# Local attention with whitening on one Trainium2 core: part of the last moments moved among the output tiles, outputs written over consumed inputs, larger stores

## The chip, the cores and the metric

The kernel runs on one core of a Trainium2 chip. The metric is device time in microseconds (us) of one execution; the kernel before has a median of 672.0 us in three runs. Profiles come from the hardware profiler, one execution each.

## What is computed

Layer 0 turns x (4 images, 256 channels, 64 x 64 pixels, float32) into 49 attention weights for each pixel and sums 49 shifted copies of x with them. Layer 1 whitens the result in groups of 64 channels.

```python
k = conv(x, w1, dilation=2, padding=6) + b1          # 256 -> 128 channels, 7x7
k = conv(k, w2) + b2                                 # 128 -> 49, 1x1
attn = softmax(k, axis=1)
y = einsum('bkchw,bkhw->bchw', 49 shifted copies of x, attn)
# layer 1: 4 groups of 64 channels, m = all pixels of all images
mean = y.mean(-1); xc = y - mean
Sigma = EPS * I + xc @ xc.T / m
rTr = 1 / trace(Sigma);  P = I
for _ in range(5):
    P = 1.5 * P - 0.5 * (P @ P @ P) @ (Sigma * rTr)
out = (P * sqrt(rTr)) @ xc * weight + bias
```

No output can be written before the moments (the sums of y and of y times y transposed) of all pixels of a channel group are known. Everything after that point is the end stage of the kernel, and the change lies around it.

## The kernel before, in words

**Layout.** Channels lie on the 128 partitions, in two channel halves, cc = 0 and cc = 1, of two groups of 64 each. An image b lies in two buffers (`slots[2*b + pr]`), one for each parity pr of the row; a buffer is `[128, cc, 32, 64]` float32, so one channel half of it is 8 KB on each partition. y is written over x in these buffers.

**Work before the end.** For most of the run TensorE computes the convolution (line 604). Attention goes by 16 steps n = (image, row parity, column parity). Each step brings a band of weights from memory (lines 1208 and 1220), turns x on TensorE (`make_blocks`, line 1264, evicted to `xb` or `xbs` and, for the edges, `xbz`, lines 1286 and 1295), sums with matmuls (`weighted_sum`, line 1328), and evicts y into the buffer (`store_y`, line 1350; for the last step `store_part`, lines 1363 and 1364). y is then turned (`turn_y`, line 1400, copied to `yt` at line 1410; for parts of the last step `turn_part`, lines 1372 and 1380) and multiplied into the moments (`moment`, line 1419, tile `sig`), 8 turned pieces of each channel half for each half of a step. LAST is step 15, `prev` step 14. The second half of `prev` is turned and summed while LAST's first half is computed: two calls of `turn_y`, four transposes each, and one call of `moments`, for both channel halves at once.

**Whitening.** `whiten(cc)` is a generator, one for each channel half. A `next` on it issues one step: mean and trace (lines 1743 to 1753), the two matmuls with `blk` and the scaled covariance (1758 to 1772), then four iterations of two steps (a product of P with P and S, copied by ScalarE to `sq` at line 1780; a product of the two halves of `sq`, taken into P by VectorE at lines 1785 and 1786), then `wmx` and the scale, then the offset: twelve `next` calls in all. The generator of cc = 0 runs first, without stop. Between its steps, `fill` takes eleven entries from `units`, a list of TensorE work on the second channel half of LAST: sums, evictions, turns, moments.

**Output tiles.** `idx` counts 33 tiles: cc = 0, then cc = 1; in each the images 3, 2, 1, 0; in each four tiles of 8 rows of each parity (the very first is split in two). A tile takes eight matmul instructions of `parts_mm` (line 1730), four for each parity, into a pair of PSUM banks. Three pairs rotate, named `apply`, `cv` and `tp` in the profile; `tp` is shared with turns and whitening steps. ScalarE evicts one parity (line 1859), VectorE the other (line 1865), with scale and offset, into a staging tile `out` (six of them rotate), and SyncE issues a store of 512 KB (line 1871), 4 KB for each partition. The two entries of `units` that are left after the first whitening, moments of LAST, come behind the matmuls of tiles 1 and 2. The second whitening starts behind tile 4 (`LEAD`) and takes one step behind the matmuls of each tile from tile 6 on.

**What sets the order.** Every TensorE instruction around the change goes through `pe(...)`, which keeps program order on TensorE. VectorE and ScalarE are ordered by the compiler's scheduler within their dependences; `tc.high_priority()` and `tc.issue_after(x)` bend this (the first step of the second whitening is held behind the two evictions of tile LEAD). Stores go in program order on SyncE.

Of the kernel before, what the change touches and what calls it, by code (L numbers as in the profile page):

```python
# [9 lines left out]
F32 = mybir.dt.float32  # L10
# [22 lines left out]
def kernel(  # L33
# [29 lines left out]
    nc = tc.nc  # L63
    B, C, H, W = x.shape
    P = 128
# [32 lines left out]
    def pe(ins):  # L98
        return tc.keep_in_program_order(ins)
# [9 lines left out]
    def tp():  # L109
        return ps_tp.tile([P, 512], F32, tag="tp", name="tp")  # L110
# [20 lines left out]
    slots = {}  # L131
    store = []

    def halves(t):

        return t.rearrange("p c r w -> p c (r w)").rearrange(
            "p c (h r w) -> p c h r w", h=2, r=SH
        )
# [3 lines left out]
    def read_x(o, k, queue):  # L142
        b, pr = divmod(k, 2)
        for cc in range(NCC):
            src = x[b, cc * P : (cc + 1) * P].rearrange("c (r two) w -> c r two w", two=2)
            for h in range(2):
                yield queue.dma_start(o[:, cc, h], src[:, :, pr, h * SW : (h + 1) * SW])  # L147
# [33 lines left out]
    t = tp()  # L181
# [3 lines left out]
    t = tp()  # L185
# [5 lines left out]
    for k in range(2):  # L191
        t = ps_cv.tile([P, 512], F32, name=f"cv{k}")
# [53 lines left out]
    for k, c0 in enumerate(range(0, P, CB)):  # L246
        n = min(CB, P - c0)
        t = cv_buf[k % 2]
# [15 lines left out]
    for k0 in range(0, KT, TB):  # L264
        n = min(TB, KT - k0)
        t = tp()
# [835 lines left out]
    def place(n):  # L1102

        b, k = divmod(n, 4)
        return (b, k % 2, k // 2) if b == B - 1 else (b, k // 2, k % 2)
# [135 lines left out]
    def tile_of(t, cc, t8, h, pc):  # L1241

        return halves(t)[:, cc, h, TR8 * t8 : TR8 * (t8 + 1), bass.ds(pc, TC, 2)]

    def turned_by(n):

        return swap if place(n)[1] else ident

    def where(n):

        b, h, pc = place(n)
        return slots[2 * b + h], pc

    upper_edge = []
    LAST = 4 * B - 1
# [107 lines left out]
                return nc.vector.tensor_scalar(o, i, shift, None, ALU.add)  # L1363
            return nc.scalar.activation(o, i, AF.Identity, bias=shift)

    def turn_part(half, cc, k, to=None, on=nc.scalar.copy):

        yt, pc = where(LAST)
        t = tp()
        for h in range(2):  # L1370
            pe(
                nc.tensor.transpose(
                    t[:, h * P : (h + 1) * P],
                    tile_of(yt, cc, 2 * half + k, h, pc),
                    turned_by(LAST),
                )
            )
        yb = yt_buf[k][:, :, cc if to is None else to]
        with tc.high_priority():
            on(yb[:, :, :, :GW], t[:, :C].rearrange("p (h g c) -> p h g c", h=2, c=GW))  # L1380
        for h in range(2):
            turned_part[half, cc, 2 * k + h] = yb[:, h]

    turned_part = {}

    def moments_part(half, cc, pieces=range(4), end=False):

        for k in pieces:
            moment(turned_part[half, cc, k], cc, end and k == 3)

    count = [0]
    ybs = {}
# [1 line left out]
    def turn_y(n, t8):  # L1394
        yt, pc = where(n)
        t = tp()
        for h in range(2):
            for cc in range(NCC):
                pe(
                    nc.tensor.transpose(  # L1400
                        t[:, h * C + cc * P : h * C + (cc + 1) * P],
                        tile_of(yt, cc, t8, h, pc),
                        turned_by(n),
                    )
                )
        yb = yt_buf[t8 % NY]
        for h in range(2):
            ybs[n, 2 * t8 + h] = yb[:, h]
        with tc.high_priority():
            return nc.scalar.copy(  # L1410
                yb.rearrange("p h a g c -> p (h a g) c")[:, :, :GW],
                t[:, : 2 * C].rearrange("p (e c) -> p e c", c=GW),
            )

    def moment(yb, cc, end=False):

        for g in range(P // GW):
            pe(
                nc.tensor.matmul(  # L1419
                    sig[g * GW : (g + 1) * GW, cc],  # L1420
                    yb[:, g, :GW],
                    yb[:, g],
                    start=(count[0] == 0),
                    stop=end,
                    skip_group_check=True,
                )
            )
        count[0] += 1

    def moments(n, half):  # L1430

        for i in range(4 * half, 4 * half + 4):
            for cc in range(NCC):
                moment(ybs[n, i][:, cc], cc)
# [149 lines left out]
    pieces = read_x(halves(store[4]), 4, nc.sync)  # L1584
# [34 lines left out]
    rpool = ctx.enter_context(tc.tile_pool(name="rp", bufs=1, reuse_waits="tile"))  # L1619
# [24 lines left out]
    n = 4 * last_b  # L1644
# [21 lines left out]
    def sums(half, cc, *ks):  # L1666
        for k in ks:
            weighted_sum(LAST, half, k, (cc,))

    prev = open_n.pop()  # L1670
    turn_y(prev, 2)
    sums(0, 0, 0)
    make_blocks(LAST, 1)
    sums(0, 0, 1)
    make_blocks(LAST, 2)
    sums(0, 0, 2)
    turn_y(prev, 3)
    sums(0, 0, 3, 4)
    stored = store_part(0, 0)
    make_blocks(LAST, 3)  # L1680
    moments(prev, 1)
    root = work.tile([P, 1], F32, tag="root", name="root")
    with tc.issue_after(stored.ins):
        nc.scalar.activation(root, cmask[:, :1], AF.Sqrt)
# [10 lines left out]
    units = [  # L1695
        lambda: sums(0, 1, 2, 3),
        lambda: (sums(0, 1, 4), store_part(0, 1)),
        lambda: sums(1, 1, 0, 1, 2),
        lambda: sums(1, 1, 3),
        lambda: (sums(1, 1, 4), store_part(1, 1, True)),  # L1700
        lambda: turn_part(0, 1, 0),
        lambda: turn_part(0, 1, 1),
        lambda: turn_part(1, 1, 0, 0),
        lambda: turn_part(1, 1, 1, 0),
        lambda: moments_part(0, 1, (0, 1)),
        lambda: moments_part(0, 1, (2, 3)),
        lambda: moments_part(1, 1, (0, 1)),
        lambda: moments_part(1, 1, (2, 3), True),
    ]


# [15 lines left out]
    def parts_mm(t, lhs, rhs, crossed=False):  # L1727
        for i, o in ((G0, G1 if crossed else G0), (G1, G0 if crossed else G1)):
            pe(
                nc.tensor.matmul(  # L1730
                    t[o], lhs[i], rhs[i], start=True, stop=True, skip_group_check=True
                )
            )
# [81 lines left out]
    chains = [whiten(cc) for cc in range(NCC)]  # L1815
# [3 lines left out]
    NT = 512  # L1819
    TR = NT // W  # L1820

    LEAD = 4
    evicted = {}

    def bank_pairs():
        while True:
            yield [ps_y.tile([P, NT], F32, tag="y", name="apply") for _ in range(2)]
            yield cv_buf
            yield [tp(), tp()]

    pair = bank_pairs()
    idx = -1
    for cc in range(NCC):
        for b in (3, 2, 1, 0):
            rows = [(q, TR) for q in range(0, SH, TR)]
            if (cc, b) == (0, B - 1):
                rows[:1] = [(0, TR // 2), (TR // 2, TR // 2)]
            for k, (r0, nr) in enumerate(rows):
                idx += 1
                st = rpool.tile([P, TR, 2, W], F32, tag="out", name=f"out_{b}_{cc}_{r0}", bufs=6)  # L1840
                st = st[:, :nr]
                ts = next(pair)
                for pr in range(2):
                    y = halves(slots[2 * b + pr])[:, cc, :, r0 : r0 + nr, :]
                    parts_mm(
                        ts[pr][:, : nr * W],
                        (wmx if pr else wm)[cc],
                        y.rearrange("p h r w -> p h (r w)"),
                        crossed=pr == 1,
                    )  # L1850
                if idx in (1, 2):
                    units.pop(0)()
                if idx > LEAD + 1:
                    next(chains[1], None)
                for pr in range(2):
                    o = st[:, :, pr, :].rearrange("p r (h w) -> p h r w", h=2)
                    i = ts[pr][:, : nr * W].rearrange("p (h r w) -> p h r w", h=2, w=SW)
                    if pr == k % 2:
                        on_act = nc.scalar.activation(
                            o, i, AF.Identity, bias=beta[cc], scale=sc[cc]  # L1860
                        )
                    else:
                        behind = evicted.get(idx - 1) if idx <= LEAD else None
                        with tc.issue_after(behind.ins) if behind else nullcontext():
                            evicted[idx] = nc.vector.tensor_scalar(
                                o, i, sc[cc], beta[cc], ALU.mult, ALU.add
                            )
                if idx == LEAD:
                    with tc.issue_after(evicted[idx].ins), tc.issue_after(on_act.ins):
                        next(chains[1])  # L1870
                nc.sync.dma_start(
                    out[b, cc * P : (cc + 1) * P, 2 * r0 : 2 * (r0 + nr), :],
                    st.rearrange("p r two w -> p (r two) w"),
                )
# [31 lines left out]
```

## Time and profile before

| what | value |
|---|---|
| median of three runs (lowest, highest) | 672.0 us (671.94, 672.1) |
| the profiled execution's own time | 671.98 us |
| its span | 670.2 us |
| granted TensorE clock, mean | 0.995 |
| PE busy in the span | 647.1 us, 97% |
| DVE, ACT busy | 566.5 us, 332.6 us |
| stores issued at line 1871 | 31 of 512 KB, 2 of 256 KB; first issued at 624.0 us, last at 663.0 us |
| packets in the window 622 to 671 on the queue of the stores | 4752, 16.78 MB |

PE is TensorE's matmuls, PEld its weight loads, DVE is VectorE, ACT is ScalarE, SPq is SyncE's queue. The span runs from the first to the last recorded event. The DMA share of a stretch is the mean busy share of the core's 16 DMA engines; it can come out slightly above 1. A view by windows gives busy time by engine in each stretch, then the granted TensorE clock, the DMA share and GB/s. The chain of waits follows the work that ended last back through what released it; with a window it is listed in order of time as start, length, what. The timeline lists instructions in order of time with, in brackets, the idle time before and what ended it. In the trace a float32 matmul shows as two instructions and a transpose as one.

### The profile page before, as it was taken

The numbers are of one execution on the slowest core, as the hardware profiler recorded it, in microseconds if no ns is written. First come the engines' busy times: TensorE is split into PE (matmuls) and PEld (weight loads), VectorE is DVE, ScalarE is ACT, GpSimd is POOL, SyncE is SP. The second block draws the span as 40 slices with busy tenths as digits, with TensorE's granted clock in tenths as the row PEclk, the third lists the DMA queues.
The fourth block names the chain that finished last, engine by engine and source line by source line (L and its number), as shares of the span: only waits on it lengthen the run. The fifth ranks groups of instructions, "written<-read, shape, count | busy, mean of one in ns | idle before, by whom it ended". The sixth has DMA issues, their size and how long they took to land.

```text
span 670.2 us, 19064 instructions
## 1 busy us (share of the span) xinstructions
PE 647.1 (97%) x7800; PEld 527.4 (79%) x7800; DVE 566.5 (85%) x1240; ACT 332.6 (50%) x862; POOL 115.0 (17%) x173
## 2 busy tenths in 40 slices
PE   6999999999999999999999999999999999999993
PEld 1439673357899998889999998999999999997430
DVE  3699999899399889999999789989999988634773
ACT  1424331023465556467755563464855566635663
POOL 0000551662203002001022020002130203500000
PEclk9999999999999999999999999999999999999998
DMA  8961899994499989313587773027374325749698
GB/s 314 251 172 66 133 242 376 218 195 68 113 195 231 209 270 314 112 53 94 167 275 246 233 276 106 2 68 193 97 189 123 71 64 117 192 103 371 255 404 347
DMA packets 110991, 126.09 MB, mean 188 GB/s; under 512 B 69255, under 2 KB 92344, under 8 KB 109752
## 3 DMA queue, kind: packets, MB, share of 16 engines
q1 hardware_dynamic: 94104, 69.35, 35.9%
q0 software_dynamic: 10752, 37.26, 21.6%
q10 hardware_dynamic: 6048, 18.27, 8.9%
q8 instruction: 61, 1.00, 0.6%
q14 instruction: 26, 0.21, 0.1%
HBM read 78.78 MB, written 52.36 MB: 196 GB/s over the span
## 4 chain that ended last, share of the span: by engine, by line
PE 83%; DVE 10%; DMA 2%; ACT 2%; issue 1%; SPq 0%; POOL 0%; DVEq 0%; ACTq 0%; POOLq 0%
PE cv L604 30%; PE y L1328 13%; PE cv L779 10%; PE acc L779 9%; PE sig L1419 5%; PE tp L1400 4%; PE tp L1264 4%; PE cv L251 2%; DMA out_dram<-out 2%; PE tp L1730 2%; DVE zz L352 1%; DVE pv L352 1%; PE tp L1021 1%; DVE zz L348 1%; DVE ct L352 1%
## 5 line engine op out<-in xcount | busy, mean ns | idle before, releaser
L604 PE MATMUL cv<-xh,wr 128*49 128x128 f32 x4160 | 232.3, 273 | 0.1
L604 PEld LDWEIGHTS cv<-xh,wr 128*49 128x49 f32 x4160 | 226.1, 124 | 2.9 <-issue 1.0
L1158 POOL DMA_DIRECT2D sd<-zt x120 | 63.0, 532 | 295.0 <-ACT zt L1139 232.0
L1328 PE MATMUL y<-band,xb 128*128 128x209 f32 x448 | 93.7, 341 | 0.6 <-ACT xb L1295 0.6
L1328 PEld LDWEIGHTS y<-band,xb 128*128 128x128 f32 x448 | 75.8, 191 | 1.4 <-ACT xb L1295 0.8
L615 ACT COPY pv<-cv 113x486 f32<-113x486 f32 (+2 forms) x60 | 26.0, 433 | 84.6 <-PE cv L604 84.2
L352 DVE SCALAR_TENSOR_TENSOR pv<-pv 113x162 f32<-113x162 f32 x176 | 53.4, 326 | 1.5 <-ACT pv L615 0.9
L1410 ACT COPY yt<-tp 128x512 f32<-128x512 f32 x60 | 35.0, 592 | 24.3 <-PE tp L1400 23.5
L1139 ACT COPY zt<-d 32x112 f32<-32x112 f32 (+2 forms) x132 | 38.6, 292 | 11.7 <-DVE d L1009 5.8
L1400 PE MATMUL tp<-ident,slot 128*128 128x128 f32 x240 | 41.3, 296 | 0.2 <-ACT slot L1350 0.2
L1061 ACT ACTIVATE d<-tp,mx 128x49 f32<-128x49 f32 x96 | 27.5, 323 | 27.4 <-DVE mx L1058 20.7
L1264 PE MATMUL tp<-ident,slot 128*128 128x128 f32 x256 | 40.5, 282 | 0.0
L1419 PE MATMUL sig<-yt 128*64 128x65 f32 x1024 | 38.0, 225 | 0.9 <-ACT yt L1410 0.9
L1400 PEld LDWEIGHTS tp<-ident,slot 128*128 128x128 f32 x240 | 34.9, 205 | 5.1 <-issue 3.8
L1264 PEld LDWEIGHTS tp<-ident,slot 128*128 128x128 f32 x256 | 38.2, 205 | 0.4 <-DMA sd<-zt 0.4
L1419 PEld LDWEIGHTS sig<-yt 128*64 128x64 f32 x1024 | 32.9, 137 | 6.8 <-issue 1.9
L1295 ACT COPY xb<-tp 128x512 f32<-128x512 f32 x52 | 30.6, 588 | 8.8 <-PE tp L1264 5.6
L779 PE MATMUL acc<-slot,tap 128*49 128x256 f32 (+7 forms) x224 | 34.7, 468 | 0.0
L352 DVE SCALAR_TENSOR_TENSOR xh<-ct 128x512 f32<-128x512 f32 x40 | 26.6, 694 | 5.7 <-PE cv L604 5.4
L779 PEld LDWEIGHTS acc<-slot,tap 128*49 128x49 f32 x224 | 16.1, 123 | 17.9 <-issue 15.5
L147 POOL DMA_DIRECT2D slot<-in_x_dram x12 | 20.4, 1699 | 53.3 <-DVE xh L352 38.2
L348 DVE TENSOR_TENSOR pv<-pv 113x162 f32<-113x162 f32 (+1 forms) x77 | 27.8, 369 | 0.3
(258 smaller groups left out, 1143.7 us busy)
## 6 DMA issues: line engine op xcount, KB each, us to landing
out_dram<-out SPq DMA_DIRECT2D x31, 512.0 KB, 5.8
band<-sd SPq DMA_DIRECT2D x64, 242.0 KB, 3.5
sd<-zt POOLq DMA_DIRECT2D x120, 77.0 KB, 3.9
wr<-gd ACTq DMA_DIRECT2D x14, 588.0 KB, 4.7
wr<-gd ACTq DMA_DIRECT2D x14, 490.0 KB, 4.4
slot<-in_x_dram POOLq DMA_DIRECT2D x12, 512.0 KB, 10.2
ahead<-in_x_dram POOLq DMA_DIRECT2D x12, 512.0 KB, 7.5
spill<-slot POOLq DMA_DIRECT2D x3, 2048.0 KB, 8.4
```

What stands on the lines that cost most here:

```text
L348: return in_turn(TT(o, a, b, ALU.subtract))
L352: return in_turn(STT(o, a, f, b, ALU.mult, ALU.add))
L604: nc.tensor.matmul(o, wv[:, sc, sr, cc], xv[bc][:, h * NCC + cc], start=(j == 0), stop=(j == len(terms) - 1), skip_group_check=True,)
L779: nc.tensor.matmul(ps[h * HB : h * HB + KT, :, o0:o1], w[v][:, cc], rhs, start=(j == 0 and k == 0), stop=(j == len(order) - 1), skip_group ...
L1139: ins = nc.scalar.copy(o, i)
L1158: dma = queue.dma_start(bass.AP(tensor=D.tensor, offset=D.offset + h * HS + g * RS, ap=[[LS, TC], [CR * RS, NCH], [1, KS * WS]],), zt[p0 : ...
L1264: nc.tensor.transpose(t[:, h * C + cc * P : h * C + (cc + 1) * P], tile_of(xt, cc, t8, h, pc), turned_by(n),)
L1295: (nc.vector.tensor_copy if n > 4 * B - 3 else nc.scalar.copy)(xb.rearrange("p a c -> p (a c)"), t[:, : 2 * C])
L1328: nc.tensor.matmul(y_ps[n, half, cc][:, q0 : q0 + nq, c0:c1], xb[:, cc * P : (cc + 1) * P], rhs, start=(k == 0), stop=(k == len(PIECES[hal ...
L1400: nc.tensor.transpose(t[:, h * C + cc * P : h * C + (cc + 1) * P], tile_of(yt, cc, t8, h, pc), turned_by(n),)
L1410: return nc.scalar.copy(yb.rearrange("p h a g c -> p (h a g) c")[:, :, :GW], t[:, : 2 * C].rearrange("p (e c) -> p e c", c=GW),)
L1419: nc.tensor.matmul(sig[g * GW : (g + 1) * GW, cc], yb[:, g, :GW], yb[:, g], start=(count[0] == 0), stop=end, skip_group_check=True,)
```

## The change

Five edits, all in the end stage:

1. Of the second half of `prev`, only the first channel half is turned and summed where it was; the second half's turns (`turn_part(1, 1, 0 and 1, n=prev)`) and moments become four more entries of `units`. The key of `turned_part` gets the step n.
2. `units` now has 17 entries. Eleven are taken in the first whitening as before; the other six are taken behind the matmuls of tiles 2 to 7: the turn by ScalarE, the turn by VectorE, two entries of LAST's moments, two of `prev`'s.
3. `LEAD` goes from 4 to 6. The second whitening starts behind tile 7 (LEAD + 1), and from tile 8 on there are two places for a step in each tile, one behind each parity's matmuls; two of every three places are used. What is left is run before cc = 1 begins.
4. Outputs of all but the first image of cc = 0 are evicted into the buffers of the image before (its channel half is consumed by then), not into the six rotating `out` tiles.
5. For cc = 1, two tiles make one store of 1 MB, 8 KB for each partition.

```diff
-    def turn_part(half, cc, k, to=None, on=nc.scalar.copy):
-        yt, pc = where(LAST)
+    def turn_part(half, cc, k, to=None, on=nc.scalar.copy, n=LAST):
+        yt, pc = where(n)
...
-            turned_part[half, cc, 2 * k + h] = yb[:, h]
+            turned_part[n, half, cc, 2 * k + h] = yb[:, h]
...
-    def moments_part(half, cc, pieces=range(4), end=False):
+    def moments_part(half, cc, pieces=range(4), end=False, n=LAST):
         for k in pieces:
-            moment(turned_part[half, cc, k], cc, end and k == 3)
+            moment(turned_part[n, half, cc, k], cc, end and k == 3)
...
     prev = open_n.pop()
-    turn_y(prev, 2)
+    turn_part(1, 0, 0, n=prev)
     sums(0, 0, 0)
...
-    turn_y(prev, 3)
+    turn_part(1, 0, 1, n=prev)
     sums(0, 0, 3, 4)
     stored = store_part(0, 0)
     make_blocks(LAST, 3)
-    moments(prev, 1)
+    moments_part(1, 0, n=prev)
...
         lambda: moments_part(0, 1, (2, 3)),
+        lambda: turn_part(1, 1, 0, n=prev),
+        lambda: turn_part(1, 1, 1, on=nc.vector.tensor_copy, n=prev),
         lambda: moments_part(1, 1, (0, 1)),
-        lambda: moments_part(1, 1, (2, 3), True),
+        lambda: moments_part(1, 1, (2, 3)),
+        lambda: moments_part(1, 1, (0, 1), n=prev),
+        lambda: moments_part(1, 1, (2, 3), True, n=prev),
     ]
...
-    LEAD = 4
+    LEAD = 6
...
-    idx = -1
+    idx, hops = -1, 0
+    free = []
     for cc in range(NCC):
+        if cc:
+            for _ in chains[1]:
+                pass
         for b in (3, 2, 1, 0):
+            outs = [
+                t.rearrange("p r w -> p (r w)").rearrange("p (r two w) -> p r two w", two=2, w=W)
+                for t in free[-2:]
+            ]
+            free += [slots[2 * b + pr][:, cc] for pr in range(2)]
...
-                st = rpool.tile([P, TR, 2, W], F32, tag="out", name=f"out_{b}_{cc}_{r0}", bufs=6)
-                st = st[:, :nr]
+                if outs:
+                    st = outs[k // 2][:, k % 2 * TR : k % 2 * TR + TR]
+                else:
+                    st = rpool.tile(
+                        [P, TR, 2, W], F32, tag="out", name=f"out_{b}_{cc}_{r0}", bufs=6
+                    )[:, :nr]
...
                         crossed=pr == 1,
                     )
-                if idx in (1, 2):
+                    if idx > LEAD + 1:
+                        if hops % 3 != 1:
+                            next(chains[1], None)
+                        hops += 1
+                if idx > 1 and units:
                     units.pop(0)()
-                if idx > LEAD + 1:
-                    next(chains[1], None)
...
-                if idx == LEAD:
+                if idx == LEAD + 1:
                     with tc.issue_after(evicted[idx].ins), tc.issue_after(on_act.ins):
                         next(chains[1])
+                if cc:
+                    if k % 2 == 0:
+                        continue
+                    st, r0, nr = outs[k // 2], r0 - TR, 2 * TR
                 nc.sync.dma_start(
```

More of the change, by code (lines that the diff above doesn't have):

```diff
@@ L1374, in turn_part @@
                     tile_of(yt, cc, 2 * half + k, h, pc),
-                    turned_by(LAST),
+                    turned_by(n),
                 )
```

## The prediction

> **What bounds the kernel now.** First the busy shares by slices: TensorE is at nine tenths nearly to the end, so up to the first store the run is TensorE's program, and after it the DMA share is high. So I read the end stage in windows of 1 us (columns: stretch, length, busy time of PE, PEld, DVE, ACT, POOL with counts, clock, DMA share, GB/s).
>
> ```profile
> 624.00:625.00 1.00, 1.00 (x16) 0.28 (x12) 0.44 (x1) 0.44 (x1) 0.00 (x0) 1.00 0.11 43
> 625.00:626.00 1.00, 1.00 (x16) 0.52 (x16) 0.67 (x1) 0.73 (x1) 0.00 (x0) 1.00 1.01 377
> 626.00:627.00 1.00, 1.00 (x16) 0.41 (x12) 0.47 (x2) 0.32 (x2) 0.00 (x0) 1.00 0.28 105
> 627.00:628.00 1.00, 1.00 (x16) 0.35 (x12) 0.82 (x2) 0.98 (x2) 0.00 (x0) 1.00 0.99 401
> ...
> 650.00:660.00 10.00, 8.98 (x60) 2.20 (x54) 6.43 (x8) 6.22 (x8) 0.00 (x0) 1.00 1.02 406
> ...
> 667.00:668.00 1.00, 0.00 (x0) 0.00 (x0) 0.00 (x0) 0.00 (x0) 0.00 (x0) 0.50 0.67 262
> ```
>
> The stores run at 406 GB/s, so 512 KB take 0.524288/0.406 = 1.291 us and all 16.78 MB 41.32 us. Bytes flow from about 624.87 (43 of 377 GB/s in the window before 625) to 667.65: 42.78 us. So the DMA engines lack work for only 1.46 us, most of it in the 626 window. The end is **first store, plus bytes over rate, plus gaps, plus 2.5 us of landing and closing**. What sets the first store is in the chain of waits:
>
> ```profile
> 602.35 0.68 PE tp L1400 x4
> ...
> 605.75 0.37 ACT xbz L1286
> 606.12 0.04 issue
> 606.17 0.46 PE y L1328 x2
> 606.63 0.49 PE tp L1264 x4
> 607.12 1.08 PE sig L1419 x32
> 608.20 0.68 PE tp L1372 x4
> ```
>
> TensorE's work, but for one wait on ScalarE's edge copies that ends at 606.17. The third view is the timeline of the output tiles:
>
> ```profile
> 623.77 0.45 PE L1419 MATMUL sig<-yt 128*64 128x65 f32 x8
> 624.15 0.65 PE L1730 MATMUL tp<-slot,PS 64*64 64x512 f32 x2
> ...
> 629.11 0.22 DVE L1753 SCALAR_TENSOR_TENSOR dg<-mu,nmu,dg 128x1 f32<-128x1 f32 x1
> 629.25 0.22 DVE L1764 SCALAR_TENSOR_TENSOR PS<-sig,eps 128x64 f32<-128x64 f32 x1
> 629.38 0.80 DVE L1865 TENSOR_SCALAR out<-tp,ab 128x512 f32<-128x512 f32 x1
> 630.10 0.80 DVE L1865 TENSOR_SCALAR out<-apply,ab 128x512 f32<-128x512 f32 x1
> 630.82 0.28 DVE L1765 SCALAR_TENSOR_TENSOR PS<-tp,mu,PS 128x64 f32<-128x64 f32 x1
> ```
>
> A store needs a tile each 1.291 us, and until about 642 tiles come each 1.2 to 1.4 us: the compute side has hardly a margin there, and whatever is put among these tiles can starve the stores. From 647 on evictions wait for stores (`out` free again); that backlog has no price.
>
> **What the Trainium skill says.** "DMA: Bandwidth & Descriptors", section "Where 436 GB/s comes from", gives 435.2 GB/s as the ceiling of the SBUF side. The trace agrees: 406 here with 4 KB rows in 512 KB, and 427.7 (mean of the windows 608 to 617) for the 2 MB loads `back<-spill` with 16 KB rows. Its section "Rules for kernel authors" asks for at least 1 MiB in a DMA; 406 at 512 KB says little is left to gain. Its section "Latency and other measured facts" has some 600 ns to the first byte; here tile 2's store issues at 626.21 and bytes come at 627.0, 0.8 us. "PSUM — Partial Sum Buffer", section "Engine vs sequencer instructions": ScalarE and VectorE are strict queues and matmuls run in program order. The trace shows it: the tile behind a whitening step waits with the step.
>
> **The change, part by part.** I work against the profiled execution: 671.98 us, span 670.2 (1.78 around it); the median is 672.0, the same within 0.1. Clock times of the new kernel are in the old clock; the shift of step 1 comes off at the end.
>
> *1. Half of `prev`'s turns and moments leave the path.* A `turn_y` is 0.47 us in the chain; the first, at 602.28, loses half: 0.235. The second stands in the wait for the edge copies and earns nothing; that wait itself starts from transposes behind the first turn, so it moves 0.235 too. The moments at 607.12 lose half of 1.08: 0.54. Sum **-0.775**, if nothing else is late: the turn at 608.20 would start at 607.43, and what it needs (ScalarE's y eviction, 606.67 to 607.40) ends at 607.17 when moved; the square-root table load and the `yt` copy behind it end near 608.95, the moments that need them come at 609.68. Both hold.
>
> *2. The units among the tiles.* No more unit behind tile 1, so tile 2 starts at once; behind tiles 2 to 7 stand two turns and four moments. Costs on TensorE: a moments unit 0.38 (623.84 to 624.22 in the chain), a tile next to other shapes 1.02, a plain tile 0.86. A turn of two transposes costs 0.235 alone and 0.44 with its change of shape in the first whitening; I take 0.44. Their copies (0.37 on ScalarE, 0.42 on VectorE) fit between evictions. Rule: an eviction ends 0.86 after its tile's matmuls (0.05 and 0.81), its store's bytes come 0.85 after that. Tile 1's matmuls end at 623.84. Tile 2: matmuls 624.86, bytes 626.57 (0.43 earlier than now). Then 0.44 + 1.02 twice and 0.38 + 1.02 three times: bytes of tiles 3 to 7 at 628.03, 629.49, 630.89, 632.29, 633.69. Each is 0.1 to 0.17 after the store before it is done: 1.40 us for a tile against 1.291. Tile 7's evictions end at 632.84, its store at 634.98.
>
> *3. The start of the second whitening.* It has one tile between its start and its first matmul now; then none. Behind tile 7's eviction VectorE needs 0.86 to line 1753 (628.47 to 629.33): 633.70. The matmul that waits for it stands between tile 8's two halves, so TensorE idles from 632.95, and the second half runs 634.05 to 634.50. Behind it are queued the rest of tile 8, all later tiles and the ScalarE eviction. Eviction to 635.36, bytes **636.21: 1.23 after the queue ran dry**. VectorE then does line 1764 (0.2), tile 8's eviction (0.8) and lines 1765 to 1772 (0.9, as 630.82 to 631.72): 635.6. The order is a guess from now, where an eviction goes ahead of 1765; the other order frees P 0.65 sooner and delays this eviction as much. So the first product in tile 9 starts at 635.75, tile 9 is evicted at 637.14, bytes **637.99, 0.49 after** the store before it.
>
> *4. The iterations.* Two of three half tiles carry a step. Per iteration: product, `sq` copy (0.27) behind whatever ScalarE evicts (0.78), product, VectorE's update (0.22) behind its eviction. Walking it through: first products at 635.75, 637.52, 639.6, 641.2, the last update at 643.05; TensorE waits once, about 0.55 in tile 11, whose bytes come at 640.83, **0.26 after** tile 10's. Then 1.2 us a tile keeps ahead of 1.291, so the six stores of tiles 11 to 16 end at 640.83 + 6 x 1.291 = 648.58. With the shift: **647.80**. Now: 667.65 - 20.66 (16 stores) = 646.99. The first half is 0.81 later although it starts 0.775 sooner.
>
> *5. Outputs over y, and the 1 MB stores.* No eviction waits for `out`, but the DMA engines were full then: nothing. Before the first 1 MB store two tiles must be out, 17 and 18, near 647.8, bytes 648.65 against 648.58: nothing. The rate: transfers of 512 KB in 1.291 us and of 2 MB in 4.903 us (2.097/0.4277), both 128 rows, give 2.2965 us per MB and 0.087 us per transfer; one of 1 MB then takes 2.495, an estimate, and eight 19.96 in place of 20.66: **-0.70**. Ends: 0 (the rows bring nothing: 0) to -0.87 (the ceiling). That is for stores where the 16 KB rows were loads, hence the lower end.
>
> *Sum.* Data ends at 647.80 + 19.96 = 667.76 against 667.65, **+0.1**; 671.98 + 0.1 = **672.1**. Not in the trace and bounded: the turns (-0.4 in all if bare, 0 as taken), the whitening's start (-0.65 to +0.5, the order on VectorE), the iterations (-0.25, no wait at all, to +2.2, below). Own range 671.1 to 673.2.
>
> **Rivals.** *The queue never runs dry (faster).* The steps and moments stay ahead of the stores, as the present order manages from 627 on. Then 671.98 - 0.775 - 0.43 (gap at 626) - 0.70 = **670.1**. For it: every engine has idle time there, and tiles are not held by `out`. Against: 1.40 us of TensorE for a tile is measured, and there is no backlog when the whitening starts.
>
> *The whitening sets the pace (slower).* An iteration takes 2.38 us now (products at 634.20, 636.60, 638.93), with two tiles in it; it is a loop through both eviction queues. If it is latency that makes it so, it still takes 2.38 with 1.5 tiles in it: 9.5 us where I walked 7.3, +2.2, less 0.65 that the 1.2 us pace had gained by tile 16: 672.1 + 1.55 = **673.6**. It decides from about 2.3 us an iteration. For it: TensorE's weight loads wait 1.0 us on P three times and 0.6 on `sq` four times now. Against: half tiles release the copies earlier.
>
> *8 KB rows earn nothing.* Step 5 at zero: **672.8**, the same within what can be told.
>
> **How the numbers follow.** A measurement of this kernel can tell about 0.2%, 1.3 us. Chances: as walked (672.1) 0.48; queue never dry (670.1) 0.27; whitening sets the pace (673.6) 0.18; rows earn nothing (672.8) 0.07. Faster by over 0.2% 0.27, within 0.48 + 0.07 = 0.55, slower 0.18. The range for 8 in 10 takes in both outer cases with 0.3 us of their own spread, 669.8 to 673.9; what lies beyond, about a third of each, is 0.15.
>
> **What would show it.** Right: first store issued near 623.3; store bytes of tile 2 near 625.8; DMA windows with under half a share at two places about 8 to 10 us behind the first store; from tile 17 on some 420 GB/s. Step 1 is wrong if the first store is not within 0.2 of 623.3, step 5 if the second half stays at 406, steps 3 and 4 if the windows of the first half show no gaps over 0.5 us (then 670) or gaps up to the second half (then 673.6). A wait for another reason, such as evictions held by reads of the buffers they overwrite, would break all of it.

## The result and the profile after

The changed kernel takes **674.84 us** (median of six runs, 674.59 to 675.08) against 672.0 before (671.76 to 672.18): 1.0042 times as long [1.0031, 1.0053]. The forecast was 672.1 and its range ended at 673.9; both lie below what was measured. The profiled execution after took 674.69 us, span 672.9, mean clock 0.993. So 2.6 us of it were not foreseen. In four of the kernels compared below, before among them, a single execution took 5 to 6.5 us longer than the rest, which the medians leave aside.

First the windows of the store stage of the kernel after (columns as in the prediction: PE, PEld, DVE, ACT, POOL, clock, DMA share, GB/s).

```profile
624.00:625.00 1.00, 1.00 (x10) 0.30 (x9) 0.70 (x1) 0.79 (x2) 0.00 (x0) 1.00 0.97 363
...
634.00:635.00 1.00, 0.98 (x8) 0.09 (x8) 0.91 (x5) 0.20 (x1) 0.00 (x0) 1.00 0.04 12
635.00:636.00 1.00, 0.95 (x8) 0.24 (x8) 0.57 (x3) 0.99 (x2) 0.00 (x0) 1.00 0.03 8
636.00:637.00 1.00, 0.48 (x10) 0.31 (x12) 0.81 (x1) 0.61 (x2) 0.00 (x0) 1.00 0.45 168
637.00:638.00 1.00, 1.00 (x14) 0.44 (x8) 0.32 (x3) 0.03 (x1) 0.00 (x0) 1.00 0.88 348
...
641.00:642.00 1.00, 0.98 (x12) 0.09 (x6) 0.90 (x3) 0.73 (x1) 0.00 (x0) 1.00 0.26 102
...
655.00:665.00 10.00, 4.55 (x44) 2.43 (x36) 4.81 (x7) 4.59 (x7) 0.00 (x0) 0.90 1.01 420
...
669.00:670.00 1.00, 0.00 (x0) 0.00 (x0) 0.00 (x0) 0.00 (x0) 0.00 (x0) 0.50 0.68 279
670.00:671.00 1.00, 0.00 (x0) 0.00 (x0) 0.00 (x0) 0.00 (x0) 0.00 (x0) 0.50 0.10 41
```

The first store comes early: a whole window is full at 624, where before bytes only began at 624.87. Then the DMA engines lie idle from about 634.05 to 636.55 (shares 0.04, 0.03, 0.45) and again at 641 (0.26). From 655 on they run at 420 GB/s; the same window before has 408:

```profile
655.00:665.00 10.00, 4.61 (x33) 1.12 (x28) 4.95 (x7) 4.71 (x7) 0.00 (x0) 0.94 1.02 408
```

I added up windows of a quarter of a microsecond to find when half of the 16.78 MB had gone: at 646.91 before and **649.60** after, 2.7 us later, although the first store is 0.84 earlier (issued at 623.21, before 624.05). From that point to the end of the span it is 23.29 and 23.30 us. So the first half of the stores loses 2.7 us net, and the second neither loses nor gains, although it has the larger stores.

The chain of waits of the kernel after (start, length, what) shows the first step of the change:

```profile
602.22 0.43 PE tp L1372 x2
...
605.80 0.46 PE y L1328 x2
606.26 0.48 PE tp L1264 x4
606.74 0.62 PE sig L1419 x16
607.36 0.68 PE tp L1372 x4
```

Half of the moments is gone (0.62 for 16 instructions, before 1.08 for 32), and the turn behind them starts at 607.36 where it was 608.20.

The third view is the timeline of the start of the second whitening (start, length, engine, line, operation, in brackets the idle time before and what ended it). Half a tile means one of its two parities. Lines of the store stage have moved: the prediction's 1730, 1753, 1764, 1786, 1859 and 1865 are now 1734, 1757, 1768, 1790, 1878 and 1884.

```profile
631.27 1.08 PE L1734 MATMUL tp<-slot,PS 64*64 64x512 f32 x4
...
632.28 0.43 PE L1762 MATMUL tp<-D,blk 128*128 128x64 f32 x2
632.40 0.81 DVE L1884 TENSOR_SCALAR slot<-tp,ab 128x512 f32<-128x512 f32 x1
633.12 0.14 DVE L1756 TENSOR_SCALAR dg<-dg 128x1 f32<-128x1 f32 x1
633.30 0.22 DVE L1757 SCALAR_TENSOR_TENSOR dg<-mu,nmu,dg 128x1 f32<-128x1 f32 x1
...
633.57 0.38 PE L1764 MATMUL tp<-dg,blk 128*128 128x1 f32 x2 [0.86 <-DVE dg L1757]
633.89 0.65 PE L1734 MATMUL tp<-slot,wmx 64*64 64x512 f32 x2
633.90 0.65 PE L1734 MATMUL apply<-back,PS 64*64 64x512 f32 x2
...
635.01 0.78 ACT L1878 ACTIVATE slot<-tp,ab 128x512 f32<-128x512 f32 x1 [0.42 <-PE apply L1734]
...
635.05 0.33 PE L1734 MATMUL tp<-PS 64*64 64x128 f32 x2
...
637.69 0.39 PE L1734 MATMUL tp<-PS 64*64 64x128 f32 x4
...
639.98 0.38 PE L1734 MATMUL tp<-PS 64*64 64x128 f32 x4
...
642.10 0.43 PE L1734 MATMUL tp<-PS 64*64 64x128 f32 x4
```

Read it from the top. Tile 8's first half (`tp<-slot,PS`) takes 1.08 us alone. Then VectorE evicts that half (632.40) **ahead of** the trace in lines 1756 and 1757, so the matmul of line 1764, which waits for the trace, starts only at 633.57. Tile 8's second half (`tp<-slot,wmx`) follows at 633.89, and tile 9's first half (`apply<-back,PS`) starts 0.01 us later and runs beside it. ScalarE's eviction of tile 8 ends at 635.79, and its store is the one that ends the gap at 636.55. Below it the rows with 64x128 are the first products of the four iterations: they come 2.64, 2.29 and 2.12 us apart, **2.35 us in the mean**.

### The profile page after: what moved, and what is told of

Its sections match the earlier page's. It is cut to its first block, busy times and chain, and to the rows that moved or that the text cites. A ratio compares the mean times of both kernels' runs of the same rounds, so it can differ in the third digit from the quotient of the medians.

```text
span 672.9 us, 19015 instructions
## 1 busy us (share of the span) xinstructions
PE 647.5 (96%) x7800; PEld 531.5 (79%) x7800; DVE 566.8 (84%) x1241; ACT 332.0 (49%) x863; POOL 115.0 (17%) x173
## 4 chain that ended last, share of the span: by engine, by line
PE 84%; DVE 10%; ACT 2%; issue 1%; DMA 1%; POOL 0%; SPq 0%; DVEq 0%; ACTq 0%; POOLq 0%
PE cv L604 30%; PE y L1328 13%; PE cv L779 10%; PE acc L779 8%; PE sig L1419 5%; PE tp L1400 4%; PE tp L1264 4%; PE tp L1734 2%; PE cv L251 2%; DVE zz L352 1%; DVE pv L352 1%; PE cv L1734 1%; PE apply L1734 1%; PE tp L1021 1%; DVE zz L348 1%
## 5 line engine op out<-in xcount | busy, mean ns | idle before, releaser
L1264 PE MATMUL tp<-ident,slot 128*128 128x128 f32 x256 | 40.5, 282 | 0.0
L1400 PE MATMUL tp<-ident,slot 128*128 128x128 f32 x232 | 39.9, 296 | 0.2 <-ACT slot L1350 0.2
```

What stands on the lines that cost most here:

```text
L1264: nc.tensor.transpose(t[:, h * C + cc * P : h * C + (cc + 1) * P], tile_of(xt, cc, t8, h, pc), turned_by(n),)
L1400: nc.tensor.transpose(t[:, h * C + cc * P : h * C + (cc + 1) * P], tile_of(yt, cc, t8, h, pc), turned_by(n),)
```

## The experiments

Medians in us, each against runs of the kernel before on the same chip. "Over" is the difference of the two medians; after itself stands at +2.84.

| kernel | median | before | over | ratio |
|---|---|---|---|---|
| e1, steps behind whole tiles | 672.69 | 671.92 | +0.77 | 1.0015 [1.0007, 1.0023] |
| e2, a step between the halves of each tile | 675.12 | 671.92 | +3.20 | 1.0047 [1.0035, 1.0060] |
| e3, trace ahead of the eviction | 674.03 | 671.92 | +2.11 | 1.0031 [1.0020, 1.0043] |
| e6, a step behind each half in turn | 675.11 | 671.92 | +3.19 | 1.0046 [1.0034, 1.0059] |
| e4, 512 KB stores | 675.15 | 671.89 | +3.26 | 1.0047 [1.0034, 1.0060] |
| e5, outputs and stores alone | 671.54 | 671.89 | -0.35 | 1.0000 [0.9990, 1.0011] |
| e9, early units | 673.99 | 671.89 | +2.10 | 1.0034 [1.0022, 1.0046] |
| e10, closer steps alone | 673.64 | 671.89 | +1.75 | 1.0025 [1.0015, 1.0036] |
| e8, e1 and e3 together | 672.28 | 671.84 | +0.44 | 1.0000 [0.9988, 1.0012] |
| e17, e8 with the end stores split | 671.85 | 671.84 | +0.01 | 1.0000 [0.9992, 1.0008] |
| e18, e5 with the end stores split | 671.46 | 671.84 | -0.38 | 1.0002 [0.9988, 1.0017] |
| e19, no iterations | 673.79 | 671.84 | +1.95 | 1.0028 [1.0018, 1.0039] |

The difference of medians and the ratio are computed differently, and the ratio of e18 falls on the other side of 1 from its medians; differences of 0.4 us and less are read here as hints only.

Three theories went in. T1: a half tile on its own costs about a whole one, because halves run in pairs and a step between them breaks the pair. T2: an iteration of the whitening keeps its length wherever its steps stand, so fewer tiles in it means slower tiles. T3: the order on VectorE, eviction ahead of trace, makes the gap at the start.

**e1, one step behind each whole tile** (after, with the placing of before):

```diff
-                    if idx > LEAD + 1:
-                        if hops % 3 != 1:
-                            next(chains[1], None)
-                        hops += 1
                 if idx > 1 and units:
                     units.pop(0)()
+                if idx > LEAD + 1:
+                    next(chains[1], None)
```

> The changed kernel, but one whitening step per tile from tile 8 on, behind both parities' matmuls, as the kernel before has it. Theory 1 (the two parities' matmuls of a tile run side by side in TensorE, 0.86 us for both; a step between them leaves a half tile alone that takes about 1.05, not 0.43): no half stands alone, the gap at the start of the second whitening falls from 2.5 to under 1 us and the one near 641 goes: 671 to 672. Theory 2 (the loop of a whitening iteration through both eviction queues takes 2.3 us wherever its steps stand; more steps per tile make it the pace): the later gaps go but the start's stays: 673.4 to 674. Theory 3 (the order on VectorE at the start, an eviction ahead of the trace): no change of the start gap: 673.4 to 674.

It takes back 2.07 of the 2.84 us, which is between the range of T1 and those of T2 and T3 and in none of them. Its iterations are as long as in after, 2.34 us in the mean (first products at 635.23, 637.56, 639.90, 642.24), but hold two tiles each: 1.17 us for a tile, where after has 2.35 / 1.5 = 1.57, and a store takes 1.29. The gap at the start shrinks too, as its windows show:

```profile
635.00:636.00 1.00, 0.92 (x16) 0.44 (x12) 0.93 (x5) 0.81 (x2) 0.00 (x0) 1.00 0.60 234
636.00:637.00 1.00, 1.00 (x18) 0.42 (x12) 0.86 (x3) 0.50 (x2) 0.00 (x0) 1.00 0.07 16
637.00:638.00 1.00, 0.94 (x16) 0.41 (x12) 0.91 (x3) 0.86 (x2) 0.00 (x0) 1.00 0.79 307
```

Shares missing from 1 add up to 1.54 us here, against 2.60 in the windows 634 to 638 of after: tile 8 is whole before the trace, and only tile 9 waits.

**e2, a step between the halves of each tile**, and **e6, behind the first half of one tile and the second of the next**. Both have two tiles in an iteration, like e1:

```diff
-                    if idx > LEAD + 1:
-                        if hops % 3 != 1:
-                            next(chains[1], None)
-                        hops += 1
+                    if idx > LEAD + 1 and pr == 0:
+                        next(chains[1], None)
```

e6 has `pr == idx % 2` in place of `pr == 0`.

> The changed kernel, but one whitening step per tile from tile 8 on, between the two parities' matmuls. The second parity of a tile then stands next to the first parity of the next, so halves still run in pairs, except in tile 8. Theory 1: the later lone halves and the gap near 641 go, the start stays: about 673.6. Theory 2: the same, since there is one step per tile: about 673.6. It is the control for the next kernel.

> The changed kernel, but one whitening step per tile from tile 8 on, in turn between the parities and behind them: as many steps as in the two kernels ahead of it, but every second tile has a half that stands alone on either side of a step. Theory 1: three groups of about 1.05 us for two tiles, 1.55 a tile against 1.291 for a store, the stores starve to tile 16: 675 or more, at least 1.5 above the control. Theory 2 (steps per tile set the pace, not their place): as the control, 673.6, within 0.5.

The two came out alike, 675.12 and 675.11, and both as slow as after. T1 wanted e6 at least 1.5 us above e2, so as a general rule **T1 falls**: where the step between them is ready, a half overlaps the next half anyway (in e6 one runs from 637.75 to 638.77 and the next from 638.12 to 639.15, with a product at 637.86 between). What fills e6's iterations is a wait of 0.32 to 0.48 us for the copy `sq` ahead of each product with `sq`. T2 missed on e2 as well: the length of an iteration is not fixed. It grew to 2.87 us in e2 (635.27, 638.12, 640.98, 643.89) and 2.76 in e6, with the same two tiles, which is 1.44 and 1.38 us for a tile, slower than the stores. Both also keep the gap of after at 634.3 to 636.7. And both show a gap at the end of the whitening, 649.4 to 651, where the steps that are left run in one go and the first 1 MB store has to wait for two tiles. In the windows 649 and 650 e2 has shares of 0.39 and 0.00, 1.6 us of idle time that after does not have; so the totals of e2 and e6 are not the price of their iterations alone, and this gap was not tried by itself.

**e3, the trace ahead of tile 8's eviction on VectorE**:

```diff
         traced = nc.vector.scalar_tensor_tensor(dg, mu, nmu, dg, ALU.mult, ALU.add)
+        traces.append(traced)
...
                         behind = evicted.get(idx - 1) if idx <= LEAD else None
+                        if idx == LEAD + 2:
+                            behind = traces[1]
```

> The changed kernel, with VectorE's eviction of tile 8 held behind the trace of the second whitening (one ordering edge, nothing else). Theory 3 (that order makes the gap at the start): the matmul that waits for the trace comes 0.7 to 0.8 us sooner, and so does all behind it, 674.0. Theory 1: 0.3 to 0.8 of it comes back, since the half tile ahead of that matmul is alone anyhow: 674.0 to 674.5. Not over 1 us by either.

Its timeline on VectorE, to be held against 632.40 to 633.52 in after (1756, 1757 and 1884 are 1758, 1759 and 1889 here):

```profile
632.42 0.15 DVE L1758 TENSOR_SCALAR dg<-dg 128x1 f32<-128x1 f32 x1
632.61 0.22 DVE L1759 SCALAR_TENSOR_TENSOR dg<-mu,nmu,dg 128x1 f32<-128x1 f32 x1
...
632.89 0.80 DVE L1889 TENSOR_SCALAR slot<-tp,ab 128x512 f32<-128x512 f32 x1
```

The trace is done 0.69 us sooner, and the kernel gains 0.73 against after: T3 holds, with its size. T1's range for this kernel holds the result too, so e3 shows what the order costs, not that the lone half costs nothing. **e8** does e1 and e3 together.

> The changed kernel with both repairs: one whitening step per tile behind both parities, and VectorE's eviction of tile 8 held behind the trace. If the two add: 672.69 (steps behind the tile) less 0.81 (what the order alone gave), 671.9. If they repair the same gap: 672.5 to 672.7.

It stands at +0.44, 0.33 less than e1 and between its two forecasts. That is a difference of the size read here as a hint: the two repairs seem to shorten in part the same gap, so that the order is worth less once tile 8 is whole before the trace.

**e10, closer steps alone**: the kernel before with edit 3's placing of steps only, LEAD still 4.

```diff
+        if cc:
+            for _ in chains[1]:
+                pass
...
+                    if idx > LEAD + 1:
+                        if hops % 3 != 1:
+                            next(chains[1], None)
+                        hops += 1
...
-                if idx > LEAD + 1:
-                    next(chains[1], None)
```

> The kernel before with the closer steps alone (whitening starts behind tile 4 as before, from tile 6 on two of every three places, one behind each parity, carry a step). Theory 2 (an iteration keeps its 2.3 us, TensorE waits with it in program order, and with 1.5 tiles in it a tile takes 1.5 us against 1.291 for a store): 1 to 2 us above before, 673 to 674, with DMA windows under 0.9 between tiles 6 and 13. Rival (the closer steps cost only at the start, where nothing stood between the trace and its matmul): at most 0.5 above before.

It costs 1.75 us with nothing else changed. The products in its timeline:

```profile
631.86 0.33 PE L1730 MATMUL tp<-PS 64*64 64x128 f32 x2 [1.08 <-DVE PS L1772]
...
633.99 0.44 PE L1730 MATMUL tp<-PS 64*64 64x128 f32 x4 [0.15 <-DVE PS L1786]
636.09 0.39 PE L1730 MATMUL tp<-PS 64*64 64x128 f32 x4
638.08 0.44 PE L1730 MATMUL tp<-PS 64*64 64x128 f32 x4
```

The first and the fourth of before, for comparison:

```profile
631.87 0.33 PE L1730 MATMUL tp<-PS 64*64 64x128 f32 x2 [1.08 <-DVE qi L1799]
...
638.93 0.33 PE L1730 MATMUL tp<-PS 64*64 64x128 f32 x2
```

An iteration is 2.07 us in the mean against 2.35 in before: closer steps do shorten it, but by 12%, while a quarter of its tiles is gone. 2.07 / 1.5 is 1.38 us for a tile. In before it was 2.35 / 2 = 1.18. The DMA shares in four of its windows (633, 634, 637, 639) are 0.76, 0.34, 0.57 and 0.79, which leaves 1.54 us idle: most of the loss. T2's total came out, its fixed length of 2.3 us did not.

**e19, no iterations** in the second whitening, on after:

```diff
-        for it in range(1, T_ITERS):
+        for it in range(1, 1 if cc else T_ITERS):
```

> The changed kernel without the four iterations of the second whitening (left out; cc = 1 is scaled with the first P). Theory 2: the gaps behind tile 9 go (about 1.3 us of idle DMA time between 637 and 647), the gap of 2.5 us at the whitening's start stays: 673.2 to 673.6. Rival: the later gaps are not the iterations but evictions into consumed buffers or the units' work: over 674.3.

It is 0.89 us better than after; 673.79 lies 0.2 above T2's range and well under the rival's 674.3. So the iterations are about a third of the 2.84 us; from 639 to 650 no window has a share under 0.99 any more, where after had 0.26 at 641. The gap at the start remains in full (shares 0.01, 0.02 and 0.52 in the windows 634 to 637).

**e4, 512 KB stores**, and **e5, outputs over y and 1 MB stores alone**. e4 is after without the block that joins two tiles; e5 is the kernel before with that block and the `outs` and `free` lines of edit 4.

```diff
-                if cc:
-                    if k % 2 == 0:
-                        continue
-                    st, r0, nr = outs[k // 2], r0 - TR, 2 * TR
```

> The changed kernel with a 512 KB store for every tile in its second half too. By the prediction's step 5 the eight 1 MB stores save 0.70 us, and the second half of the trace runs near 418 GB/s with them and near 406 without: 675.5 (674.84 + 0.7). If the row size earns nothing: 674.8.

> The kernel before with two of the five edits alone: outputs over consumed y, and 1 MB stores for cc = 1. By step 5: 0.7 below before, 671.2 to 671.4. If the evictions over y bring waits of their own or the rows earn nothing: 671.9 or more.

The row of e4's windows for the second half, beside 420 in after:

```profile
655.00:665.00 10.00, 4.69 (x44) 2.51 (x36) 4.96 (x7) 4.75 (x7) 0.00 (x0) 0.91 1.02 406
```

The rate is what the prediction said, 420 GB/s (422 in e5) against 406. But the clock shows only 0.42 (after against e4) and 0.35 (e5 against before) of the 0.70, each about the size of a hint. From half of the bytes to the end of the span the traces agree: 23.65 us in e4 and 23.30 in after, 23.29 in before and 22.96 in e5. Part of what is missing seems to lie behind the last bytes. In before the bytes end at 667.65 and the span at 670.2, 2.5 us on. The last windows of e5:

```profile
666.00:667.00 1.00, 0.00 (x0) 0.00 (x0) 0.00 (x0) 0.00 (x0) 0.00 (x0) 0.50 0.48 197
667.00:668.00 1.00, 0.00 (x0) 0.00 (x0) 0.00 (x0) 0.00 (x0) 0.00 (x0) 0.50 0.08 33
```

0.48 and 0.08 put the last byte at 666.56, and its span ends at 669.5, 2.9 us on; in after it is 3.1 (669.78 to 672.9). But 1 MB stores alone do not make this longer. The last windows of e4, which has 512 KB stores to the end:

```profile
670.00:671.00 1.00, 0.00 (x0) 0.00 (x0) 0.00 (x0) 0.00 (x0) 0.00 (x0) 0.50 0.55 217
671.00:672.00 1.00, 0.00 (x0) 0.00 (x0) 0.00 (x0) 0.00 (x0) 0.00 (x0) 0.50 0.04 16
```

They put its last byte at 670.59, and its span ends at 673.4, 2.8 us on; and e1, e2 and e6, with the 1 MB stores of after, have only 2.2 to 2.3. To see whether the size of the last store makes a difference on the clock, **e18** (on e5) and **e17** (on e8) split the first and the last 1 MB store in two:

```diff
-                if cc:
+                if cc and (b, k // 2) not in ((3, 0), (0, 1)):
```

> The kernel before with outputs over y and 1 MB stores, the first and last split into 512 KB. If the late landing of the last 1 MB store took half of the 0.70 us of step 5: 671.54 less 0.2 to 0.35, 671.2 to 671.35, the best version. If not: 671.5 to 671.6.

> As the kernel ahead of it, and the first and the last 1 MB store each split into two of 512 KB. The first of cc = 1 then doesn't wait for a second tile where the queue is dry (a gap of 0.7 us at 647.7 with steps behind the tile), and the last lands as quickly as before (1 MB stores end some 0.35 us later after their last bytes): 0.4 to 0.9 below it, about 671.2. If the gap is the whitening's end and not the pairing of tiles: only the 0.35 of the landing.

e18 stands at -0.38, as e5 does at -0.35: nothing came back, although 2.7 us lie behind its last bytes where e5 has 2.9. So the size of the last store is not shown to be the cause, and with e4 and e1 it is unlikely to be. e17 gained 0.43 over e8, less than the 671.2 it was to reach, but there the first 1 MB store was short of tiles, which the split relieves too: the share in the window 647 is 1.05, in e8 0.60, and 2.3 us lie behind its last bytes, in e8 2.6. How much of the 0.43 each is worth is not told apart.

**e9, early units**: e8 with two units behind each tile from tile 1 on and LEAD = 3, so that the whitening starts while stores are still ahead.

```diff
-    LEAD = 6
+    LEAD = 3
...
-                if idx > 1 and units:
-                    units.pop(0)()
+                for _ in range(2):
+                    if idx > 0 and units:
+                        units.pop(0)()
```

> The changed kernel with the six units in pairs behind tiles 1 to 3, the whitening begun behind tile 4 with one step per tile behind both parities, and the eviction order of the earlier experiment: the changed kernel's shorter path to the first store with the old cadence. If the four moved units are paid in full among the tiles (2.2 us of TensorE at a stage with no margin): 0.84 sooner and some 1.5 to 2 later than the outputs-and-stores kernel, 672 to 672.5. If they hide under the stores: 670.4 to 670.8, the best version.

It missed both forecasts: +2.10, worse than e8's +0.44. Its profiled execution, 675.11, the highest of its five (the others 673.82 to 674.11), shows one thing that no other profile here does:

```profile
632.00:633.00 1.00, 0.01 (x2) 0.04 (x2) 0.93 (x5) 0.45 (x1) 0.00 (x0) 1.00 1.02 406
633.00:634.00 1.00, 1.00 (x10) 0.47 (x12) 0.53 (x3) 0.27 (x1) 0.00 (x0) 0.64 0.86 340
634.00:635.00 1.00, 1.00 (x11) 0.42 (x7) 0.00 (x0) 0.00 (x0) 0.00 (x0) 0.50 0.68 262
635.00:636.00 1.00, 1.00 (x13) 0.39 (x10) 0.75 (x2) 0.78 (x1) 0.00 (x0) 0.50 0.02 8
636.00:637.00 1.00, 1.00 (x15) 0.43 (x11) 0.20 (x3) 0.00 (x0) 0.00 (x0) 0.65 0.07 29
```

TensorE waits 1.42 us for VectorE, and then its clock is 0.50 to 0.65 for over 3 us, with the stores dry behind it. Whether the four shorter executions had this too, no trace says, so what early units cost by themselves stays open.

**What was left over.** e1 and e8 differ from e5 by the moved half (edits 1 and 2) and the later start of the whitening with its remaining placing. e8 is 0.79 above e5 and e1 is 1.12 above, although the half that is moved makes the first store 0.86 (e8) and 0.68 (e1) us sooner than in before. So about 1.6 to 1.8 us are given back later, more than the path gained, by the moved work among the tiles and the late start of the whitening together; the two were not tried apart. No version here beats the kernel before by more than the measurement tells.

## Why the prediction was wrong

The profiled execution took 674.69, the forecast was 672.1. In the forecast's own terms the 2.6 us are made up as follows.

| term of the sum | predicted | measured | difference |
|---|---|---|---|
| queue idle from first bytes to tile 7's store | 1.07 | 0.95 | -0.1 |
| gap at the start of the whitening | 1.23 + 0.49 = 1.72 | 2.45 | +0.73 |
| gaps in the iterations up to half of the bytes | 0.26 | 1.48 | +1.22 |
| from half of the bytes to the end of the span | 19.96 + 2.5 = 22.5 | 23.30 | +0.8 |

Measured idle times are lengths on the clock less the bytes that went, at 406 GB/s; the first store was issued within 0.07 of its forecast.

*Step 1, right.* The first store is issued at 623.21, forecast near 623.3; the chain shows the half moments at 0.62 and the half turn at 0.43, where before had 1.08 and 0.68. (The text of the step has 0.47 for a whole turn, the line that it shows has 0.68.)

*Step 2, right.* Tiles 3 to 7 start their matmuls at 624.28, 625.73, 627.14, 628.54 and 629.94, 1.40 to 1.45 us apart where 1.40 to 1.46 was walked; shares there are 0.73 to 1.01 and the queue runs dry at 634.05, forecast 634.2 in the new clock.

*Step 3 failed* in two places, and both can be read in the timeline of after. "The second half runs 634.05 to 634.50" costs a half tile at half of a tile. The two parities of a tile are matmuls of 64x64 in different quarters of the array (`crossed=pr == 1` in the kernel), and they run side by side: both together take 0.86 to 1.02 here in a row of tiles, so one alone, at 1.08, is no cheaper. The Trainium skill has the rule in "TensorEngine Tiling (Array Packing)", section "Key Properties": tiles of the array run matmuls in parallel, and a change of tiling mode drains the engine. The trace agrees with the first (633.89 and 633.90 start together); the price of the drain no run here shows, and the gap doesn't need it: in program order tile 8's second half stands behind the matmuls of lines 1762 and 1764, and the latter waits for the trace. The other place is the order on VectorE. The guess of the step was whether an eviction goes ahead of the line then numbered 1765. That one could go ahead of the trace itself it put at nothing (0.86 us to the trace with nothing between), and this is what happened. In the new clock the trace was to end at 632.93 and ended at 633.52, +0.59; the half took 0.63 more; tile 8 was evicted at 635.79 and not at 634.59. Tile 9 had run beside it and was then ready in time, so its own 0.49 gap did not come. e3 confirms the order's part alone with -0.73.

*Step 4 failed, with the largest term.* The walk put the first products 1.6 to 2.1 us apart; they came 2.64, 2.29 and 2.12 apart. It took 7.3 us for four iterations with 1.5 tiles each, 1.2 us for a tile, one wait of 0.55 included. The timeline of after shows what stands in the first two iterations instead:

```profile
635.07 0.65 PE L1734 MATMUL apply<-slot,wmx 64*64 64x512 f32 x2
635.55 0.60 PE L1734 MATMUL apply<-slot,wmx 64*64 64x512 f32 x2
636.67 0.27 PE L1734 MATMUL tp<-sq 64*64 64x64 f32 x2 [0.52 <-ACT sq L1784]
...
637.91 1.02 PE L1734 MATMUL tp<-back,PS 64*64 64x512 f32 x4
638.95 0.27 PE L1734 MATMUL tp<-sq 64*64 64x64 f32 x2
638.97 0.65 PE L1734 MATMUL tp<-slot,wmx 64*64 64x512 f32 x2
639.12 0.60 PE L1734 MATMUL apply<-back,PS 64*64 64x512 f32 x2
```

Between the two products of each of them one half tile stands alone (635.07 to 636.15, 637.91 to 638.93; in the third 639.88 to 640.90), 1.02 to 1.08 us, because the product with `sq` comes behind it in program order and is not ready before. The other two halves run side by side in 1.1 to 1.2 us. So 1.5 tiles take TensorE nearly as long as two whole ones do: e1, with two whole tiles in an iteration, has 2.34 us. On top comes one wait, 0.52 us for `sq`. The 1.2 us for a tile leave no room for that, so this looks like the mistake of step 3 again, a half tile taken for half of a tile.

The rival that the whitening sets the pace had put the turning point at 2.3 us and the price at +1.55; measured are 2.35 us and +1.22 (by the gaps; leaving the iterations out in e19 gains 0.89). So its length came out, but its reason only in part. It took the length of the loop for fixed, and that was 2.07 us in e10, 2.34 in e1 and 2.87 in e2; that after has just the 2.35 of before is chance. The waits of TensorE's weight loads on which it leaned, for P and for `sq`, don't tell the kernels apart: over the four iterations they add up to 4.9 us in before, 5.6 in after and 6.2 in e1, whose DMA shares from 638 to 647 are 0.98 and more. In after the copy `sq` of the second iteration is done at 638.90 and the lone half at 638.93, so which of the two holds TensorE can't be read from this trace, and no run here changes one without the other. The argument against the rival, that half tiles release the copies earlier, is true in a small way (2.07 us in e10 where before had 2.35), but a loop with a quarter of its tiles gone would have needed 1.94 to keep up with the stores (1.5 x 1.291). What goes with the gaps in these kernels is the iteration divided by the tiles in it, against 1.29 us for a store: 1.17 in e1 keeps ahead; 1.38 to 1.57 in e10, e6, e2 and after does not.

*Step 5, the mechanism right and the size half.* 420 GB/s was said and measured. The term was -0.70; the two comparisons give -0.42 and -0.35, so the rival that the rows earn nothing falls with the rate and is half right on the clock. The time behind the last bytes, carried over from before at 2.5 us, was 3.1 in after; but it was 2.8 in e4 with 512 KB stores and 2.2 to 2.3 in e1, e2 and e6 with 1 MB ones, and what it goes by stays open. e4, with the stores of before, already takes 23.65 us for its second half where before takes 23.29: of the +0.8 in the table, about 0.35 is the rate that did not reach the clock and as much stands in e4 too. Outputs over y at nothing is consistent with e5, where both edits together gain 0.35. The lower end of this step's range, -0.87 "(the ceiling)", doesn't follow from the 435.2 GB/s that it names: 8.39 MB at that rate are 19.28 us, -1.38 against 20.66. Nothing hangs on it here.

The rival "queue never dry" fell with the gap at 634. Its argument against, no backlog when the whitening starts, was the right one.

## What to carry to other kernels

Price a small serial chain that is woven into a stream of tiles by the loop time that the trace shows, divided by the tiles in one loop, and compare that with the time of one transfer. This is a first estimate only: the loop moved between 2.07 and 2.87 us here as its steps were placed otherwise. Matmuls that run in different parts of the array together can't be costed at a half each; a step that has to wait and stands between them can make one half cost as much as the pair. And before work is moved from a busy path into a stage that feeds a full DMA queue, count that stage's margin: here 0.7 to 0.9 us came off the front, and in e1 and e8 some 1.6 to 1.8 were given back afterwards.

## What the hardware showed that was not expected

- A half tile of four 64x64 float32 matmul records took 1.08 us alone, and 1.08 together with the half of another tile beside it (633.89 to about 634.97).
- After a wait of 1.42 us on TensorE the granted clock fell to 0.50 for a time (e9, one profile), while it stayed at 1.00 through waits of 1.08 us in before, 0.86 in after and 0.85 in e1. What the clock goes by is not shown.
- With 1 MB stores of 8 KB rows the queue ran at 418 to 422 GB/s against 406 to 408 with 512 KB and 4 KB rows. Only about half of what that rate promises came off the clock.
- The time from the last bytes to the end of the span was 2.5 us in before and 2.8 in e4 (512 KB stores), 2.2 to 2.3 in e1, e2 and e6 and 2.9 to 3.1 in e5 and after (1 MB stores).
